# A four-layer graph network: layer 2's self loops put into memory, blocks of its normalisation moved, and the order of layer 3's edge loop changed

## The chip, the cores and the metric

The kernel runs on one core of one Trainium2 chip. The metric is the device time of one launch in microseconds (us). The core's engines are TensorE (PE; its weight loads, PEld, run beside its matmuls), VectorE (DVE), ScalarE (ACT), GpSimd (POOL) and SyncE (SP). Each takes its own instructions in the order in which they were issued and waits on semaphores for what another engine or a transfer has to deliver.

## The reference

A graph of 3125 nodes with 256 features runs through four layers. Each layer normalises x, adds to x the output of a graph attention and of a second mixing branch, and then adds the output of a gated network of experts ("ffn"). There are 50,000 random pairs taken in both directions and one self loop for each node, so 103,125 edges, sorted by target. Two of the attentions matter here.

```python
# layer 2, 4 heads of 64: attention over the edges and, once more, over self loops
src = concatenate([edge_index[0], loop]); dst = concatenate([edge_index[1], loop])
alpha = leaky_relu(a_s[src] + a_d[dst], 0.2)           # per edge and head
coef = softmax of alpha over the edges of one dst
out = relu(segment_sum(coef[:, :, None] * h[src], dst) + bias)
y = out + x
return (y - mean) * rsqrt(var + 1e-5) * gamma + beta   # per node

# layer 3, 8 heads of 32: three terms per edge, each of 4 kinds, weighted by an edge mask
e = (left(src, mask) + right(dst, mask) + em(edge_attr_16, mask)) / 3.0
e = where(e > 0, e, 0.2 * e)
a = softmax of e over the edges of one dst
rst = segment_sum(feat_src[src] * a[:, :, None], dst)
```

## The kernel before

**Units.** Nodes are taken in 25 tiles of 125 (`TP` = 125, `NT` = 25) as targets and in 25 tiles of 128 (`NS`) as sources. The edges stand in 806 columns of 128 (`NE`, `P`), sorted by target. Layers 0 to 2 do their attention densely: a matrix of edge counts, `count_d`, one byte for each pair of source and target, is built once in memory, and `weigh` (L2058) multiplies a tile of it by the exponentials of the scores.

**Layer 2, `dense`.** Four chunks of targets, (0, 6), (6, 6), (12, 6) and (18, 7) in tiles, each go over 25 source tiles. A step loads a tile of counts (`count_tile`, L2064), adds the identity where the tile crosses the diagonal (L2072, because layer 2 counts each self loop once more than the graph has it), makes four weighted tiles on DVE (L2061), and multiplies them on PE (L2316, L2321). Work of the chunk before is woven in, one piece at a step (`next(work, None)`): first `turned`, the transposing and scaling of its tiles, then `gnn2_blocks` (L1297), the addition, normalisation and residual for three or four tiles at a time. PE, DVE and ACT are in an order written out by hand there. The blocks of the last chunk are returned as `tail` and run within the expert network of layer 2 (FFN2, `ffn2` from L1396), three pieces after each expert of the first group of tiles. FFN2 also calls `between()` once, which works on weights of layer 3.

**Layer 1's second attention**, which has one head, runs in the loop `go`, over seven groups of targets (`ONES`) and 25 source tiles. It reads the same `count_d`, and it is the last reader of it before layer 2.

**Layer 3, `edge_attention`.** Here work goes by edges: 101 steps (`steps`) of eight columns (`SC`), the last with six. `columns(t)` (L1842) gives for each target tile the range of columns in which its edges may lie: the range that even spacing gives, with a margin of four columns at both sides. `here[i]` lists the target tiles, one or two, whose range meets step i. The parts of a step are:

- `load`: target numbers (`row`), edge features (`ef`) and masks by DMA on SP's queue, three steps ahead.
- `gather` (L2592): eight indirect DMAs on POOL's queue bring the rows of the sources into `z_edge` (four buffers).
- `targets` (L2605): for each tile of the step, DVE compares target numbers with node numbers into `hot`, which has two buffers.
- `products` (L2617, L2620): PE sums the edge features' term and `er` times `hot` into `p_m`; ACT copies it to `m_sb` (L2622).
- `turn` (L2627): PE transposes `m_sb` into `p_e`.
- `weights` (L2635 to L2651): on DVE `l`, twice, and `e`, twice; ACT's exponential `near_e` (L2643); DVE's one-hot matrices `oh` (L2647, three buffers); and DVE's multiplication of the gathered rows by the weights, in place in `z_edge` (L2651).
- `sums` (L2660): PE multiplies `oh` and `z_edge` column by column into `p_acc`, one accumulator for a target tile.
- `divide`: DVE divides a finished tile by its sum and adds it to x.

The loop over i issues load(i+3), products(i), sums(i-2), gather(i+1), weights(i-1), targets(i+1), divide(i-2) and turn(i), with two calls of `piece()` between, which bring in work of layer 3's mixing branch and its expert network as it becomes ready. PE and DVE take this order as it is written (`manual_schedule`); ACT's order is left to the scheduler.

Of the kernel before, what the change touches and what calls it, by code (L numbers as in the profile page):

```python
# [2 lines left out]

# [60 lines left out]
class Net:  # L64
# [1231 lines left out]

    def gnn2_blocks(self, x, xn, att, weights, t0, nt):  # L1297

        nc = self.nc
        for b in range(t0, t0 + nt, 3 if nt == 6 else 4):  # L1300
            n = min(3 if nt == 6 else 4, t0 + nt - b)
            gamma, beta = (r[:, None, :].to_broadcast([TP, n, C]) for r in weights)
            a, xs = att[:, b:b + n, :], x[:, b:b + n, :]
            nc.vector.tensor_add(a, a, xn[:, b:b + n, :])
            nc.gpsimd.tensor_add(xs, xs, beta)
            yield
            mv = self.moments(a, (0, n))
            yield
            rstd = self.norms.tile([TP, 4], F32, name="rstd")
            nc.scalar.activation(rstd[:, :n], mv[:, :n, 1], AF.Sqrt, bias=self.eps5[:TP], scale=1.0)  # L1310
            yield
            nc.vector.reciprocal(rstd[:, :n], rstd[:, :n])
            back = self.norms.tile([TP, 4], F32, name="back")
            nc.vector.scalar_tensor_tensor(back[:, :n], mv[:, :n, 0], -1.0, rstd[:, :n], op0=OP.mult, op1=OP.mult)
            for t in range(n):
                nc.scalar.activation(a[:, t, :], a[:, t, :], AF.Identity, bias=back[:, t:t + 1], scale=rstd[:, t:t + 1])
            yield
            nc.vector.tensor_mul(a, a, gamma)
            nc.vector.tensor_add(xs, xs, a)
            yield  # L1320
# [75 lines left out]
    def ffn2(self, x, xn, xT, weights, tail=None, between=None):  # L1396
        nc, tc = self.nc, self.tc
        E = 8
        with ExitStack() as s:
# [56 lines left out]
            def aside(i, e):  # L1456
                if i + 1 < len(GROUPS):
                    t0, nt = GROUPS[i + 1]
                    if e == 0:
                        mv[i] = self.moments(x, GROUPS[i + 1])  # L1460
                    if e == 1:
                        self.normed(xn, x, GROUPS[i + 1], mv[i])
                    if e == 2:
                        self.transposed(ps, xT, xn, groups=[GROUPS[i + 1]])
                    if e == 3:
                        raw[i] = self.exponents(ws, self.scores(ws, ps, xT[:, :, t0 * TP:(t0 + nt) * TP], nt, wr, br))
                    if e == 4:
                        wfs[i + 1] = self.shares(ws, raw[i])
                if e == 5:
                    turn_weights(i)  # L1470
                if e == 6:
                    add_biases(i)
                if tail and i == 0:
                    for _ in range(3):
                        next(tail, None)
                if between and (i, e) == (1, 4):
                    between()
# [144 lines left out]
class Dense(Net):  # L1622
# [219 lines left out]
    def columns(self, t):  # L1842

        return max(0, t * TP * 33 // P - MARGIN), min(NE, -(-(t + 1) * TP * 33 // P) + MARGIN)

# [217 lines left out]

    def count_tile(self, w, t, d0, n, loops, width=875):  # L2064
        nc = self.nc
        K = min(P, N - t * P)
        a = w.tile([P, width], U8, name="a")
        nc.sync.dma_start(a[:K, :n], self.count_d[t, :K, d0:d0 + n])
        if loops:
            lo, hi = max(t * P, d0), min(t * P + K, d0 + n)  # L2070
            if lo < hi:
                nc.vector.tensor_add(a[:K, lo - d0:hi - d0], a[:K, lo - d0:hi - d0], self.ident[:K, lo - t * P:hi - t * P])  # L2072
        return a, K

    def dense_pairs(self, att, nodes, then):
# [7 lines left out]
        with ExitStack() as s:  # L2083
# [48 lines left out]
            def near_counts(n):  # L2132
                c, _ = near[n // NS]
                counts[n] = self.count_tile(wa, n % NS, c * TP, nq, False, nq)

# [116 lines left out]

    def dense(self, nodes, scaled, then, finish=None, loops=False, early=None, first=None, onward=None, **side):

# [5 lines left out]
        with ExitStack() as s:  # L2260
# [36 lines left out]
            with tc.manual_schedule(engines={mybir.EngineType.PE, mybir.EngineType.DVE, mybir.EngineType.Activation}):  # L2297
                for i in (0, 2):
                    ask(0, i)
                for c, (t0, nt) in enumerate(chunks):  # L2300
# [5 lines left out]
                    for t in range(NS):  # L2306
                        a, K = self.count_tile(wa, t, d0, n, loops)
                        pts = [self.weigh(wp, qs[i][:K, :n], bar[:K, t, i:i + 1], a, n, K) for i in range(4)]
# [44 lines left out]
    def attention_one(self, x, xT, name, slope, w, load):  # L2353
# [51 lines left out]
        def onward(wq, wa, wp, wo, ps1, ps):  # L2405
# [34 lines left out]
            def weighed(i, t):  # L2440
                t0, nt = ONES[i]
                a, K = self.count_tile(wa, t, t0 * TP, nt * TP, False)
                pts[i, t] = self.weigh(wp, qs[i][:K, :nt * TP], bar[:K, t:t + 1], a, nt * TP, K), K
# [14 lines left out]

            def go(work):
                order = [(i, t) for i in (0, 1) for t in range(ready)] + [(i, t) for i in (0, 1) for t in range(ready, NS)]  # L2460
                order += [(i, t) for i in range(2, len(ONES)) for t in range(NS)]
# [3 lines left out]
                for at in range(len(order) + 4):  # L2465
# [3 lines left out]
                    if at < len(order):  # L2469
# [4 lines left out]
                        if i and t == 14:  # L2474
                            if i == 2:
                                load()
                            if i + 1 < len(ONES):
                                ask(i + 1)
# [10 lines left out]
                    next(work, None)  # L2489
                for _ in work:  # L2490
                    pass
# [34 lines left out]
    def edge_attention(self, x, xT, weights, pieces, then):  # L2526
# [10 lines left out]
        with ExitStack() as s:  # L2537
# [25 lines left out]
            nc.gpsimd.iota(node_sb, pattern=[[TP, NT]], base=0, channel_multiplier=1, allow_small_or_imprecise_dtypes=True)  # L2563
            nc.vector.tensor_copy(node, node_sb)
            work = [pieces(wt, pst)]

# [41 lines left out]
            def products(i):  # L2608

                p_m = ps.tile([P, 2 * P], F32, name="p_m")  # L2610
                for t in [None] + here[i]:
                    for q in range(4):
# [6 lines left out]
                        elif strips(i, t)[0] <= q < strips(i, t)[1]:  # L2619
                            nc.tensor.matmul(p_m[s, :], er[:, t, :], hots[i, t][:, qs], start=False, stop=(t == last))  # L2620
                terms[i] = w.tile([P, 2 * P], F32, name="m_sb")
                nc.scalar.activation(terms[i], p_m, AF.Copy)  # L2622

# [54 lines left out]
            last = len(steps)  # L2678
            with tc.manual_schedule(engines={mybir.EngineType.PE, mybir.EngineType.DVE}):
                for i in range(3):  # L2680
# [3 lines left out]
                for i in range(last + 2):  # L2684
                    if i + 3 < last:
                        load(i + 3)
                    if i < last:
                        products(i)
                    if i >= 2:
                        sums(i - 2)  # L2690
                    if i + 1 < last:
                        gather(i + 1)
                    if 1 <= i <= last:
                        weights(i - 1)
                    piece()
                    if i + 1 < last:
                        targets(i + 1)
                    if i >= 2:
                        divide(i - 2)
                    if i < last:  # L2700
                        turn(i)
                    piece()
                while work:
                    piece()
# [490 lines left out]
    def layers(self, x, xn, xT, out, late):  # L3195
# [55 lines left out]
        with tc.tile_pool(name="node2", bufs=1) as ap:  # L3251
            nodes = self.beside(ap, "g2", xT, 4, 0.2, lambda work: self.mix2(x, xn, xT, work, gw[-1]), self.row(ap, "L2_gnn_bias", P))
            tail = self.dense(nodes, lambda t, p, inv: self.gnn2_scaled(att, t, p, inv),
                              lambda t0, nt, ps: self.gnn2_blocks(x, xn, att, gw, t0, nt), loops=True,
                              early=lambda ps: self.ffn2_first(x, xn, xT, ps))
# [147 lines left out]
```

## Time and profile before

| | |
|---|---|
| median of 10 runs | 5135.85 us (5129.56 to 5148.08) |
| the profiled execution's own time | 5138.03 us |
| its span | 5136.2 us |
| mean granted PE clock | 0.948 of full speed |
| busy share of the span | PE 91%, PEld 55%, DVE 66%, ACT 32%, POOL 30% |
| layer 1's one-head loop | about 2150 to 2400 us |
| layer 2's dense loop | 2818 to 3257 us, chunks of 98.9, 107.0, 108.8 and 123.7 us |
| FFN2 | 3257 to 3838 us |
| layer 3's edge loop | 3876 to 4934 us |
| end of layer 3 | to 5136 us |

The span is that of one profiled execution, from the first to the last instruction; all durations are from it. "Busy" leaves out the time in which an engine waits. In rows of the profile `out<-in` gives the tiles that an instruction writes and reads, "x" how many there were, and "idle before" the time in which the engine stood still ahead of them, with what ended it. L with a number is a line of the kernel before.

### The profile page before, as it was taken

How to read it: one execution, taken by the hardware profiler on the slowest of the kernel's cores; microseconds unless marked ns; L12 is line 12 of the kernel's file. 1: busy time of each engine (PE TensorE's matmuls, PEld its weight loads, DVE VectorE, ACT ScalarE, POOL GpSimd, SP SyncE). 2: the span in 40 equal slices, each digit the busy share in tenths (PEclk: the TensorE clock that was granted, in tenths of full speed). 3: DMA queues.
4: the chain of work that ended last, by engine and by line, in shares of the span. 5: the costliest groups of instructions: out<-in, count | busy, mean ns of one | idle time of the engine just before them, and what ended most of it. 6: DMA issues, size and time to landing. Idle time of an engine off the chain costs nothing. (4 is left out here: it accounts for less than half of the span.)

```text
span 5136.2 us, 74838 instructions
## 1 busy us (share of the span) xinstructions
PE 4654.4 (91%) x28141; PEld 2824.8 (55%) x28141; DVE 3387.1 (66%) x5768; ACT 1666.2 (32%) x2861; POOL 1521.3 (30%) x1413
## 2 busy tenths in 40 slices
PE   6798999969899899999998999999996787889878
PEld 4564433448656444488555433455664565555567
DVE  6988887855635888755334999522236887777843
ACT  2668877731243011110332011233331102323221
POOL 1107866824300000000001000000006777777733
PEclk8899999979999999999999999999998898999989
DMA  4866544532300111121000111200005566666645
GB/s 94 82 59 168 161 126 142 145 114 65 103 1 3 40 42 38 31 46 38 3 16 23 32 42 31 71 10 0 1 18 158 164 184 179 169 178 173 192 140 172
DMA packets 351142, 443.50 MB, mean 86 GB/s; under 512 B 145052, under 2 KB 270256, under 8 KB 350329
## 3 DMA queue, kind: packets, MB, share of 16 engines
q1 hardware_dynamic: 266790, 222.80, 17.9%
q0 software_dynamic: 55024, 175.53, 12.0%
q10 hardware_dynamic: 28959, 40.29, 2.5%
q8 instruction: 228, 3.74, 0.3%
q14 instruction: 141, 1.15, 0.1%
HBM read 384.87 MB, written 56.78 MB: 86 GB/s over the span
## 5 line engine op out<-in xcount | busy, mean ns | idle before, releaser
L2061 DVE SCALAR_TENSOR_TENSOR pt<-q_head,bar,a 128x750 f32<-128x750 f32 (+4 forms) x975 | 889.1, 964 | 154.3 <-PE acc L2448 88.2
L2592 POOL DMA_INDIRECT z_edge<-tab,src_i x806 | 774.8, 961 | 303.9 <-issue 209.8
L2316 PE MATMUL acc<-pt,zs 128*32 128x375 f32 (+1 forms) x6400 | 637.1, 496 | 22.4 <-DVE pt L2061 14.5
L2187 POOL TENSOR_TENSOR pt_far<-pt_far,a_far 128x1125 f32<-128x1125 f32 (+1 forms) x200 | 476.4, 2383 | 277.1 <-DMA a<-count_d 147.7
L2660 PE MATMUL p_acc<-z_edge,oh 128*125 128x264 f32 x2044 | 525.3, 416 | 3.1 <-DVE z_edge L2651 3.1
L2142 DVE SCALAR_TENSOR_TENSOR pt<-q_here,bar,a 128x1000 f32<-128x1000 f32 (+1 forms) x384 | 455.8, 1249 | 46.3 <-DMA a<-count_d 17.7
L2660 PEld LDWEIGHTS p_acc<-z_edge,oh 128*125 128x125 f32 x2044 | 405.8, 203 | 131.0 <-issue 41.6
L2156 PE MATMUL p_n<-pt,zs 128*64 128x500 f32 (+1 forms) x1600 | 404.6, 597 | 28.5 <-DVE pt L2142 28.2
L2316 PEld LDWEIGHTS acc<-pt,zs 128*32 128x32 f32 x6400 | 224.5, 110 | 349.0 <-issue 246.9
L2321 PE MATMUL acc<-pt,zs 128*32 128x375 f32 (+2 forms) x3200 | 352.2, 491 | 0.0
L1436 DVE SCALAR_TENSOR_TENSOR x<-p_y,sm,x 125x256 f32<-125x256 f32 x200 | 96.6, 483 | 381.0 <-PE p_y L751 381.0
L2448 PE MATMUL acc<-xn,pt 128*125 128x257 f32 (+1 forms) x1250 | 283.5, 382 | 10.5 <-DVE pt L2061 9.9
L2448 PEld LDWEIGHTS acc<-xn,pt 128*125 128x125 f32 (+1 forms) x1250 | 229.3, 187 | 56.8 <-DVE pt L2061 14.7
L2156 PEld LDWEIGHTS p_n<-pt,zs 128*64 128x64 f32 (+1 forms) x1600 | 155.2, 137 | 190.6 <-issue 93.9
L1420 ACT ACTIVATE h<-p_tr,bn 128x500 f32<-128x500 f32 (+1 forms) x224 | 161.4, 722 | 296.5 <-PE p_tr L751 296.5
L2201 PE MATMUL p_f<-pt_far,zs 128*64 128x375 f32 (+1 forms) x1200 | 244.2, 489 | 8.5 <-POOL pt_far L2187 8.3
L2185 ACT ACTIVATE pt_far<-q_log,log_s 128x1125 f32<-128x1125 f32 (+1 forms) x200 | 244.8, 1224 | 20.4 <-PE p_f L2201 17.4
L2186 ACT ACTIVATE pt_far<-pt_far,log_s 128x1125 f32<-128x1125 f32 (+1 forms) x200 | 247.1, 1235 | 6.5
L2651 DVE TENSOR_TENSOR z_edge<-z_edge,near_e 128x2112 f32<-128x2112 f32 (+1 forms) x101 | 236.4, 2341 | 16.0 <-ACT near_e L2643 15.9
L2620 PE MATMUL p_m<-hot,er 125*32 125x256 f32 x1046 | 103.5, 445 | 141.9 <-DVE hot L2605 140.4
L2321 PEld LDWEIGHTS acc<-pt,zs 128*32 128x32 f32 (+1 forms) x3200 | 127.1, 109 | 154.4 <-issue 147.1
L2647 DVE SCALAR_TENSOR_TENSOR oh<-near,dst_f 128x1000 f32<-128x1000 f32 (+2 forms) x149 | 153.3, 1044 | 63.2 <-PE p_acc L2660 63.2
(583 smaller groups left out, 7466.1 us busy)
## 6 DMA issues: line engine op xcount, KB each, us to landing
a<-count_d SPq DMA_DIRECT2D x384, 125.0 KB
a_far<-far_d SPq DMA_DIRECT2D x96, 281.2 KB
row<-dst_row SPq DMA_DIRECT2D x101, 224.0 KB
a<-count_d SPq DMA_DIRECT2D x144, 93.8 KB
ef<-in_edge_s SPq DMA_DIRECT2D x101, 128.0 KB
z_edge<-tab,src_i POOLq DMA_INDIRECT x806
count_d<-stage SPq DMA_DIRECT2D x12, 781.2 KB
q_head<-q_g ACTq DMA_DIRECT2D x24, 375.0 KB
```

Of the source, the lines that this page charges most:

```text
L2061: self.nc.vector.scalar_tensor_tensor(pt[:K, :n], q, bar, a[:K, :n], op0=OP.max, op1=OP.mult)
L2142: nc.vector.scalar_tensor_tensor(pt[:K], q[:K], bar[:K, t, h:h + 1], a[:K].rearrange("p (j n) -> p j n", j=2), op0=OP.max, op1=OP.mult)
L2156: nc.tensor.matmul(accs[u][64 * j:64 * j + 64, :M * TP], zs[:K, t, h * W:h * W + 64], pt[:K, j, :], start=(t == 0), stop=(t == NS - 1))
L2185: nc.scalar.activation(f[:K], logs[u, i][:K], AF.Relu, bias=log_s[:K, 0, t, h])
L2186: nc.scalar.activation(f[:K], f[:K], AF.Exp, bias=log_s[:K, 1, t, h], scale=1.0 - 0.2)
L2187: nc.gpsimd.tensor_tensor(f[:K], f[:K], a[:K], OP.mult)
L2201: nc.tensor.matmul(far_accs[u][b][64 * i:64 * i + 64, :n], zs[:K, t, z:z + 64], fs[i][:K, b * n:(b + 1) * n], start=(t == 0), stop=(t == N ...
L2316: nc.tensor.matmul(acc[i // 2][r:r + 32, b, :b1 - b0], zs[:K, t, i * W + f:i * W + f + 32], pts[i][:K, b0:b1], **st)
L2321: nc.tensor.matmul(acc[2][32 * i:32 * i + 32, b, :b1 - b0], zs[:K, t, z:z + 32], pts[i][:K, b0:b1], **st)
L2448: nc.tensor.matmul(banks[i, j], pt[:K, j * TP:(j + 1) * TP], zs[:K, t, :], start=(t == 0), stop=(t == NS - 1))
L2592: nc.gpsimd.indirect_dma_start(out=zs[i][:, j, :], out_offset=None, in_=table, in_offset=bass.IndirectOffsetOnAxis(ap=src[:, c0 + j:c0 + j ...
L2660: nc.tensor.matmul(acc[t], ohs[i, t][:, k - a, :], zs[i][:, k - c0, :HW], start=(k == cols[t][0]), stop=(k == cols[t][1] - 1))
```

## The change

- **Self loops of layer 2.** `count_tile` adds the identity no more. `add_loops` loads the diagonal blocks of `count_d` in the one-head loop of layer 1, at group 2, adds the identity to them at group 4 and stores them after that loop. The counts in memory then have layer 2's self loops.
- **Blocks of layer 2's normalisation.** Which blocks run behind which chunk is now a table: (9, 3), (12, 3) and (15, 3) go into the tail. The tail runs in FFN2, three pieces after each expert of the first group and two of the second; `between()` is called after the eighth expert of the second group in place of the fifth, with the rest of the tail ahead of it.
- **Columns.** The margin of `columns` is computed from the spread of the edges' places, two to four columns.
- **Layer 3's loop.** `sums(i - 2)` stands ahead of `products(i)`, and `targets(i + 1)` ahead of `weights(i - 1)`. The copy to `m_sb` is a part of its own, `copied(i)`, behind `weights(i - 1)`. A one-element exponential (`soon`) ends each step. ACT's order is by hand here too.

```diff
@@ -1294,11 +1295,10 @@
         for i in range(4):
             nc.scalar.activation(att[:, t, i * 64:(i + 1) * 64], p[:, i // 2, 64 * (i % 2):64 * (i % 2) + 64], AF.Relu, scale=inv[:, i:i + 1])
 
-    def gnn2_blocks(self, x, xn, att, weights, t0, nt):
-
-        nc = self.nc
-        for b in range(t0, t0 + nt, 3 if nt == 6 else 4):
-            n = min(3 if nt == 6 else 4, t0 + nt - b)
+    def gnn2_blocks(self, x, xn, att, weights, t0):
+
+        nc = self.nc
+        for b, n in {0: ((0, 3), (3, 3)), 6: ((6, 3),), 18: ((9, 3), (12, 3), (15, 3), (18, 4), (22, 3))}.get(t0, ()):
             gamma, beta = (r[:, None, :].to_broadcast([TP, n, C]) for r in weights)
             a, xs = att[:, b:b + n, :], x[:, b:b + n, :]
             nc.vector.tensor_add(a, a, xn[:, b:b + n, :])
...
@@ -1470,10 +1470,12 @@
                     turn_weights(i)
                 if e == 6:
                     add_biases(i)
-                if tail and i == 0:
-                    for _ in range(3):
+                if tail and i < 2:
+                    for _ in range(3 if i == 0 else 2):
                         next(tail, None)
-                if between and (i, e) == (1, 4):
+                if between and (i, e) == (1, 7):
+                    for _ in tail:
+                        pass
                     between()
 
             order = [(i, e) for i in range(len(GROUPS)) for e in range(E)]
...
@@ -1841,7 +1843,10 @@
 
     def columns(self, t):
 
-        return max(0, t * TP * 33 // P - MARGIN), min(NE, -(-(t + 1) * TP * 33 // P) + MARGIN)
+        def margin(b):
+            return min(MARGIN, max(2, math.ceil(3.2 * math.sqrt(32 * TP * b * (NT - b) / NT) / P)))
+
+        return max(0, t * TP * 33 // P - margin(t)), min(NE, -(-(t + 1) * TP * 33 // P) + margin(t + 1))
 
     def counts(self, pieces, later):
 
...
@@ -2061,16 +2066,28 @@
         self.nc.vector.scalar_tensor_tensor(pt[:K, :n], q, bar, a[:K, :n], op0=OP.max, op1=OP.mult)
         return pt
 
-    def count_tile(self, w, t, d0, n, loops, width=875):
-        nc = self.nc
+    def count_tile(self, w, t, d0, n, width=875):
         K = min(P, N - t * P)
         a = w.tile([P, width], U8, name="a")
-        nc.sync.dma_start(a[:K, :n], self.count_d[t, :K, d0:d0 + n])
-        if loops:
-            lo, hi = max(t * P, d0), min(t * P + K, d0 + n)
-            if lo < hi:
-                nc.vector.tensor_add(a[:K, lo - d0:hi - d0], a[:K, lo - d0:hi - d0], self.ident[:K, lo - t * P:hi - t * P])
+        self.nc.sync.dma_start(a[:K, :n], self.count_d[t, :K, d0:d0 + n])
         return a, K
+
+    def add_loops(self, w):
+
+        nc = self.nc
+        whole = N // P
+        left = N - whole * P
+        a = w.tile([P, NS, P], U8, name="own_a")
+        own = (a[:, :whole, :], dview(self.count_d, 0, [[N, P], [P * N + P, whole], [1, P]]))
+        last = (a[:left, whole, :left], dview(self.count_d, whole * (P * N + P), [[N, left], [1, left]]))
+        for rows, at in (own, last):
+            nc.gpsimd.dma_start(rows, at)
+        yield
+        nc.vector.tensor_add(own[0], own[0], self.ident[:, None, :].to_broadcast([P, whole, P]))
+        nc.vector.tensor_add(last[0], last[0], self.ident[:left, :left])
+        yield
+        for rows, at in (own, last):
+            nc.gpsimd.dma_start(at, rows)
 
     def dense_pairs(self, att, nodes, then):
 
...
@@ -2457,6 +2474,7 @@
                     nc.vector.scalar_tensor_tensor(x[:, t0 + j, :], acc[:, :C], inv, x[:, t0 + j, :], op0=OP.mult, op1=OP.add)
 
             def go(work):
+                own = self.add_loops(w)
                 order = [(i, t) for i in (0, 1) for t in range(ready)] + [(i, t) for i in (0, 1) for t in range(ready, NS)]
                 order += [(i, t) for i in range(2, len(ONES)) for t in range(NS)]
                 both = [b for k in range(3) for b in half(k)]
...
@@ -2474,6 +2492,8 @@
                         if i and t == 14:
                             if i == 2:
                                 load()
+                            if i in (2, 4):
+                                next(own)
                             if i + 1 < len(ONES):
                                 ask(i + 1)
                     for i, a, b in ends.pop(at, ()):
...
@@ -2487,7 +2507,7 @@
                         if t == NS - 1:
                             ends.setdefault(at + 2, []).append((i, a, b))
                     next(work, None)
-                for _ in work:
+                for _ in chain(work, own):
                     pass
 
             return go
...
@@ -2562,6 +2582,7 @@
             node_sb = w.tile([TP, NT], F32, name="node")
             nc.gpsimd.iota(node_sb, pattern=[[TP, NT]], base=0, channel_multiplier=1, allow_small_or_imprecise_dtypes=True)
             nc.vector.tensor_copy(node, node_sb)
+            soon = wt.tile([1, 1], F32, name="soon")
             work = [pieces(wt, pst)]
 
             def piece():
...
@@ -2618,8 +2639,12 @@
                                              start=True, stop=(last is None))
                         elif strips(i, t)[0] <= q < strips(i, t)[1]:
                             nc.tensor.matmul(p_m[s, :], er[:, t, :], hots[i, t][:, qs], start=False, stop=(t == last))
-                terms[i] = w.tile([P, 2 * P], F32, name="m_sb")
-                nc.scalar.activation(terms[i], p_m, AF.Copy)
+                terms[i] = p_m
+
+            def copied(i):
+                m_sb = w.tile([P, 2 * P], F32, name="m_sb")
+                nc.scalar.activation(m_sb, terms[i], AF.Copy)
+                terms[i] = m_sb
 
             def turn(i):
                 p_e = ps.tile([P, 2, P], F32, name="p_e")
...
@@ -2676,7 +2701,7 @@
 
 
             last = len(steps)
-            with tc.manual_schedule(engines={mybir.EngineType.PE, mybir.EngineType.DVE}):
+            with tc.manual_schedule(engines={mybir.EngineType.PE, mybir.EngineType.DVE, mybir.EngineType.Activation}):
                 for i in range(3):
                     load(i)
                 gather(0)
...
@@ -2684,22 +2709,26 @@
                 for i in range(last + 2):
                     if i + 3 < last:
                         load(i + 3)
+                    if i >= 2:
+                        sums(i - 2)
                     if i < last:
                         products(i)
-                    if i >= 2:
-                        sums(i - 2)
                     if i + 1 < last:
                         gather(i + 1)
+                    if i + 1 < last:
+                        targets(i + 1)
                     if 1 <= i <= last:
                         weights(i - 1)
+                    if i < last:
+                        copied(i)
                     piece()
-                    if i + 1 < last:
-                        targets(i + 1)
                     if i >= 2:
                         divide(i - 2)
                     if i < last:
                         turn(i)
                     piece()
+                    if i < last:
+                        nc.scalar.activation(soon, self.eps5[:1], AF.Exp)
                 while work:
                     piece()
```

The calls of `count_tile` and `gnn2_blocks` drop their last argument.

More of the change, by code (lines that the diff above doesn't have):

```diff
@@ L2 @@
 from itertools import chain
+import math
 import numpy as np
@@ L2133, in near_counts @@
                 c, _ = near[n // NS]
-                counts[n] = self.count_tile(wa, n % NS, c * TP, nq, False, nq)
+                counts[n] = self.count_tile(wa, n % NS, c * TP, nq, nq)
             def near_weigh(n):
@@ L2251, in dense_pairs, with dense @@
                     ends = [e for e in ends if next(e, self) is not self]
-    def dense(self, nodes, scaled, then, finish=None, loops=False, early=None, first=None, onward=None, **side):
+    def dense(self, nodes, scaled, then, finish=None, early=None, first=None, onward=None, **side):
         nc, tc = self.nc, self.tc
@@ L2306, in dense @@
                     for t in range(NS):
-                        a, K = self.count_tile(wa, t, d0, n, loops)
+                        a, K = self.count_tile(wa, t, d0, n)
                         pts = [self.weigh(wp, qs[i][:K, :n], bar[:K, t, i:i + 1], a, n, K) for i in range(4)]
@@ L2441, in weighed @@
                 t0, nt = ONES[i]
-                a, K = self.count_tile(wa, t, t0 * TP, nt * TP, False)
+                a, K = self.count_tile(wa, t, t0 * TP, nt * TP)
                 pts[i, t] = self.weigh(wp, qs[i][:K, :nt * TP], bar[:K, t:t + 1], a, nt * TP, K), K
@@ L3253, in layers @@
             tail = self.dense(nodes, lambda t, p, inv: self.gnn2_scaled(att, t, p, inv),
-                              lambda t0, nt, ps: self.gnn2_blocks(x, xn, att, gw, t0, nt), loops=True,
+                              lambda t0, nt, ps: self.gnn2_blocks(x, xn, att, gw, t0),
                               early=lambda ps: self.ffn2_first(x, xn, xT, ps))
```

## The prediction

> **What bounds the kernel now.** Only two stretches of the program are touched for long: layer 2's dense loop (2818 to 3257 us, the four chunks of twenty-five steps) and layer 3's edge loop (3876 to 4934 us, 101 steps). I read first the busy times in windows cut at those borders, the columns being window, length, then busy us and instructions of PE, PEld, DVE, ACT and POOL, the granted PE clock, the DMA share and GB/s.
>
> ```profile
> core 0: us, PE busy (x) PEld busy (x) DVE busy (x) ACT busy (x) POOL busy (x), PEclk, DMA share, GB/s
> 2818.10:2917.00 98.90, 98.68 (x1204) 42.43 (x1207) 95.91 (x107) 1.71 (x4) 0.00 (x0) 0.98 0.16 48
> 2917.00:3024.00 107.00, 105.99 (x1226) 41.44 (x1226) 103.82 (x141) 13.19 (x39) 0.00 (x0) 1.00 0.14 38
> 3024.00:3132.80 108.80, 107.06 (x1224) 40.81 (x1225) 104.59 (x141) 11.89 (x38) 0.00 (x0) 1.00 0.14 40
> ...
> 3876.40:4933.60 1057.20, 882.68 (x5028) 600.13 (x5027) 811.40 (x1187) 246.71 (x466) 777.23 (x812) 0.91 0.61 172
> ```
>
> In the dense chunks PE and DVE are both nearly full: the second and third chunk are 8.1 and 9.9 us longer than the first, and DVE's busy time grew by 7.9 and 8.7 with them. DVE work added there is paid almost one to one. In the edge loop nobody is full: a step is 1057.2/101 = 10.47 us, PE is busy 83% of it, DVE 77%, POOL 74%. Second, then, POOL's waits around that stretch (total us, times, longest).
>
> ```profile
> POOL z_edge L2592 <- issue: 209.8, 688, 0.4
> ...
> POOL z_edge L2592 <- PE p_acc L2660: 16.2, 26, 3.2
> ```
>
> POOL's gathers set the pace: 806 of them, each 0.96 us busy and 0.30 of "issue", 1.26 x 8 = 10.1 us a step, and their waits for freed buffers are small (11 are over 0.3 us, 20.8 us together). Third, the groups by line, for the prices (busy us, mean ns, then idle before and what ended it).
>
> ```profile
> L2660 PE MATMUL p_acc<-z_edge,oh 128*125 128x264 f32 x2044 | 525.3, 416 | 3.1 <-DVE z_edge L2651 3.1
> ...
> L2651 DVE TENSOR_TENSOR z_edge<-z_edge,near_e 128x2112 f32<-128x2112 f32 (+1 forms) x101 | 236.4, 2341 | 16.0 <-ACT near_e L2643 15.9
> L2605 DVE TENSOR_TENSOR hot<-row,near 125x1024 f32<-125x1024 int16 (+3 forms) x148 | 156.1, 1081 | 0.0
> L2647 DVE SCALAR_TENSOR_TENSOR oh<-near,dst_f 128x1000 f32<-128x1000 f32 (+2 forms) x149 | 153.3, 1044 | 63.2 <-PE p_acc L2660 63.2
> L2620 PE MATMUL p_m<-hot,er 125*32 125x256 f32 x1038 | 102.9, 445 | 140.7 <-DVE hot L2605 139.2 <-DVE z_edge L2651 1.1
> ...
> L2617 PE MATMUL p_m<-ef,attn_m 16*32 16x256 f32 x800 | 65.6, 399 | 0.0
> ...
> L2640 DVE TENSOR_REDUCE e<-l 128x64 f32<-128x256 f32 (+1 forms) x101 | 60.9, 603 | 3.5
> ...
> L2638 DVE TENSOR_TENSOR l<-l,mask 128x256 f32<-128x256 f32 (+1 forms) x101 | 43.1, 427 | 3.5
> L2635 DVE TENSOR_TENSOR l<-p_e,z_edge 128x256 f32<-128x256 f32 (+1 forms) x101 | 42.4, 420 | 81.1 <-PE p_acc L2660 24.2 <-DMA z_edge<-tab,src_i 21.4 <-PE p_e L2627 21.2
> ...
> L2641 DVE SCALAR_TENSOR_TENSOR e<-e 128x64 f32<-128x64 f32 (+1 forms) x101 | 23.0, 228 | 3.5
> ```
>
> The 0.0 behind L2605 is the row that matters most: today `hot` never waits on DVE. PE waits 139.2 us for `hot`, up to 7.4 at a time, under POOL's pace.
>
> **Three blocks of layer 2 into FFN2.** Blocks (9,3), (12,3), (15,3) leave chunks three and four. A block costs DVE 0.95 for the first add, 3 x (0.40 + 0.18) for the moments, 0.33 for reciprocal and shift, 1.91 for the last two operations: 4.94 us, three are 14.8. Paid one to one by the windows above: -15 (bounds -8, were PE's near-full share the real limit, and -22 with the loops below). In FFN2 PE is busy 567.6 of 581.5 us, so what is hidden there is hidden by PE; but its `p_tr` waits for ACT's `h` four times, 9.1 us, where the two present blocks run. Five blocks: +2 (0 to +5). `between()` only runs three steps later; its result is read after 3838.
>
> **Self loops.** The 27 recorded adds of L2072 at 0.26 to 0.28 us (7 us of DVE over four chunks) go. The first chunk, with seven of them, has PE at 98.7 of 98.9 us, so I count 0 for them. In their place come two loads and two stores on POOL's queue and one add of 3072 elements in the one-head loop (2150 to 2400 us). By the 128x750 row (0.96 us) the add is about 4 us, an estimate; PE is busy 239.7 of those 250 us and weighted tiles are made ahead, so 0, at worst +4. POOL is idle there (0.35 us busy), and the stores have 400 us to land.
>
> **Narrower columns.** 1022 pairs of edge column and tile become 1002, 523 strips 513, 149 pairs of step and tile 146, all at the first and last five tiles. A pair costs PE 525.3/1022 = 0.51 us and DVE 0.15: -10 us of PE, -6 of DVE with the strips. Alone this is hidden by POOL's pace; it enters the chain below as about -0.15 us a step.
>
> **Exponentials.** A dummy Exp at the end of each step draws the table load (L2643, 35 loads of 1283 ns) out of the path from `e` to the multiplication by `near_e`. The trace prices that path's loss at 15.9 us of DVE waiting in the whole loop, under POOL's pace; so 0, at best -16. The Trainium skill's "ScalarE: Activation LUTs", section What ACT_TABLE_LOAD costs, gives 2.66 us for each switch with its drain; 35 of them would make this part -93. The waits of this trace say that most of that is covered already.
>
> **The order in layer 3's loop.** Iteration i on PE is now sums(i-2), products(i), turn(i); on DVE it is targets(i+1), weights(i-1), divide(i-2). Either swap shortens a wait that is there: PE's 139.2 us for `hot`. Together they close a loop, because `hot` has two buffers. Where steps i and i+1 have more than two tiles between them, which is so for 69 of the 100 neighbouring pairs ((1,2) 24, (2,1) 24, (2,2) 21), a `hot` of step i+1 needs a buffer that products(i) reads. Products(i) stand on PE behind sums(i-2). And queued behind the waiting `hot` on DVE are l, l, e, e, oh and the multiplication of step i-1, on which sums(i-1) wait, and behind these products(i+1). Before, targets came after weights and products before sums, so none of this was a circle. In the changed kernel's instruction order 137 of 146 `hot` wait for PE (84 of 149 before).
>
> One turn of the circle, from the rows above: DVE 156.1 + 42.4 + 43.1 + 60.9 + 23.0 + 153.3 + 236.4 = 715.2, or 7.08 us a step; PE 525.3 + 102.9 + 65.6 = 693.8, or 6.87 us; together 13.95, with the narrower columns 13.8, against 10.47 now. 69 x 13.8 = 952. The other 31 steps lie between DVE's busy time (811.4/101 = 8.0 us) and POOL's pace and its present slack (10.3): 248 to 319, and I take the middle, 285. The loop: 1237, +180 (ends 1200, +143, and 1271, +214). What is late next is POOL: its gathers wait for z_edge buffers that sums release, and lose nothing more by it.
>
> PE becomes idler, and here its clock counts. The trace: 3876 to 4355 us, PE 77% busy, clock 0.88; 4600 to 4917, 89% busy, 0.96. At (882.7 - 10)/1237 = 71% the nearest row is 0.88, perhaps 0.87: 0.91/0.87 on 6.87 us is 0.3 a step, 69 times, up to +22, which goes to the upper end. The Trainium skill's "TensorE: Matmul & The Clock Gate", section Part 1: The HAM clock gate, halves the clock after an idle window of about 3.4 us and needs as long to warm up. DVE's part of the circle is 7 us, so by this rule every such step would start cold and lose some 1.7 us, +117 in all. The trace already has pauses of up to 7.4 us (the waits for `hot`) and 0.88 beside them, and speaks for the smaller figure.
>
> **Sum.** -15 + 2 + 0 + 0 + 180 = +167. The profiled execution took 5138.03 us (span 5136.2), 2.2 above the median of 5135.85, well inside the spread of the runs (5129.56 to 5148.08): 5136 + 167 = 5303 us.
>
> **Rivals.** (A) The circle doesn't decide, and the loop falls onto POOL's pace: its waits go (-20.8) and some 5 us of the tail behind the last gather, which is 16 us now: 5136 - 26 - 13 = 5097, faster. For it speaks that POOL bounds today and that PE has 17% of slack; it decides if a step's wait of `hot` stays under about 10.3 - 8.0 = 2.3 us. Against it, sums and products alone are 6.87 us. (B) The circle closes in part: only the second `hot` of a step waits and the first (1.08 us) slips out, and products of the first tile run early; 12.0 to 13.8 us for 69 steps with 8.0 for the rest is 1076 to 1200, +19 to +143 less 13: 5142 to 5266, middle 5200. (C) The circle closes and takes in other work: the pieces of layer 3's hidden layer (DVE 811 - 715 = 96 us, two thirds of it in closed steps, 65) and the colder clock (22): 5303 + 87 = 5390. For it: ACT is in hand order too, so `m_sb` of step i stands behind near_e of step i-1. (D) The narrow columns miss an edge and the general path runs: in the given inputs tile 2's first edge lies in column 63 and its range starts at 61, and so for the rest; chance nil.
>
> **Chances.** The forecast 0.72, C 0.12, B 0.10, A 0.06. A measurement of this kernel tells about 0.2%, 10 us, from no change; A is faster by more, a small part of B within it. The range leaves out A, the lower half of B and what lies above C: 5200 to 5390.
>
> **What would show it.** Right: the loop is near 1240 us; `hot`, 0.0 now, waits hundreds of us on DVE for PE's products; sums wait over 100 us for the multiplied z_edge (3.1 now); gathers wait for sums in most steps, 150 us or more; the loop's clock is at or under 0.88; chunks three and four are near 104 and 114 us. Wrong: `hot` waits under 2.3 us a step and the gathers keep 1.26 us. If chunks three and four don't shorten, or FFN2 grows by over 5 us, the smaller terms are wrong.

## The result

The changed kernel takes 5377.32 us (median of 8 runs, 5371.31 to 5384.18) where the kernel before takes 5138.06 (28 runs): ratio 1.0464, interval 1.0455 to 1.0473, 239 us slower. The forecast was 5303 us, 165 above before, with a range up to 5390: direction and mechanism held, and the loss was half as large again.

The windows of the changed kernel, cut at the same borders (window, length, busy us of PE, PEld, DVE, ACT and POOL, clock, DMA share, GB/s):

```profile
core 0: us, PE busy (x) PEld busy (x) DVE busy (x) ACT busy (x) POOL busy (x), PEclk, DMA share, GB/s
2814.70:2912.10 97.40, 97.35 (x1204) 56.08 (x1207) 94.91 (x102) 1.71 (x4) 0.00 (x0) 0.98 0.16 48
2912.10:3019.00 106.90, 105.91 (x1226) 41.41 (x1223) 102.44 (x134) 13.20 (x39) 0.00 (x0) 1.00 0.14 38
3019.00:3122.00 103.00, 102.54 (x1226) 40.57 (x1226) 98.69 (x123) 10.03 (x34) 0.00 (x0) 1.00 0.15 42
3122.00:3236.40 114.40, 114.37 (x1220) 41.71 (x1218) 106.52 (x117) 8.37 (x30) 0.00 (x0) 1.00 0.08 22
3855.70:5172.90 1317.20, 988.15 (x4969) 661.67 (x4969) 806.67 (x1182) 245.27 (x560) 776.82 (x812) 0.83 0.48 138
```

The dense chunks are 1.5, 0.1, 5.8 and 9.3 us shorter, 16.7 together. From the end of the dense loop to the first gather it was 619.9 us (3256.5 to 3876.4) and is 619.3 (3236.4 to 3855.7), so FFN2 swallows its three blocks. The edge loop, from the first gather to the last division, was 1057.2 us and is 1317.2 (3855.7 to 5172.9): +260. The rest, ahead of the dense loop and behind the edge loop, is -4.5, and the sum, +238, is the difference of the spans (5136.2 and 5374.4). In the last line above the loop's work is what it was (POOL 777 us for 777, DVE 807 for 811), PE is busy 105 us longer with less of it, and the clock fell from 0.91 to 0.83.

The waits of the changed kernel in that loop (total us, times, longest):

```profile
engine line waited for: us in total, times, longest us
...
DVE hot L2626 <- PE p_m L2641: 426.1, 75, 13.6
POOL z_edge L2613 <- PE p_acc L2685: 287.3, 73, 10.8
...
PE p_e L2652 <- ACT m_sb L2646: 181.1, 74, 10.6
...
PE p_acc L2685 <- DVE z_edge L2676: 99.5, 62, 3.0
```

`hot`, which never waited, waits 75 times and 426 us for products; the gathers wait 73 times for sums, 287 us where it was 16; the sums wait 99.5 us for the multiplied `z_edge`, where it was 3.1. These are the three arcs of one circle. One turn of it can be read off the timeline (start, us, engine, line, operation, and in brackets the idle time before with its releaser):

```profile
start us, us, engine line op out<-in xcount [idle before <-releaser]
4310.03 2.34 DVE L2676 TENSOR_TENSOR z_edge<-z_edge,near_e 128x2112 f32<-128x2112 f32 x1
...
4312.43 5.87 PE L2685 MATMUL p_acc<-z_edge,oh 128*125 128x264 f32 x16 [2.11 <-DVE z_edge L2676]
...
4318.23 0.63 PE L2638 MATMUL p_m<-ef,attn_m 16*32 16x256 f32 x8
...
4318.80 1.07 PE L2641 MATMUL p_m<-hot,er 125*32 125x256 f32 x10
4319.53 2.35 DVE L2626 TENSOR_TENSOR hot<-row,near 125x1024 f32<-125x1024 int16 x2 [5.60 <-PE p_m L2641]
...
4323.49 1.19 DVE L2672 SCALAR_TENSOR_TENSOR oh<-near,dst_f 128x1000 f32<-128x1000 f32 x1
...
4324.25 0.69 PE L2652 MATMUL p_e<-ident,m_sb 128*128 128x128 f32 x2 [4.38 <-ACT m_sb L2646]
4324.60 2.34 DVE L2676 TENSOR_TENSOR z_edge<-z_edge,near_e 128x2112 f32<-128x2112 f32 x1
...
4327.00 0.80 PE L2685 MATMUL p_acc<-z_edge,oh 128*125 128x264 f32 x1 [2.06 <-DVE z_edge L2676]
```

The multiplication ends at 4312.4, the sums start at once and end at 4318.3, the products follow and release both `hot` after 5.60 us of waiting, then come l, l, e, e, `oh` and the next multiplication, which ends at 4326.9: 14.6 us a turn, and at no moment of it do PE's sums and DVE's chain run side by side. PE stands idle for 4.4 us ahead of the transposes and for 2.1 us ahead of the sums. Its granted clock in the same turn, cut where it changes (columns as in the windows above):

```profile
4309.80:4316.60 6.80, 4.69 (x12) 3.31 (x13) 4.03 (x7) 0.00 (x0) 4.83 (x6) 0.50 0.96 304
4316.60:4323.40 6.80, 3.27 (x26) 1.64 (x24) 3.77 (x6) 0.00 (x0) 3.91 (x4) 1.00 0.62 181
4323.40:4330.20 6.80, 3.89 (x9) 2.77 (x10) 3.54 (x3) 0.61 (x3) 3.91 (x5) 0.50 0.52 154
```

The clock is whole or half, and the sums of this turn and of the next begin at half. From the first to the last gather it stands at half in 65 stretches, 457 of 1293 us; in the kernel before in 29 stretches, 181 of 1041 us.

I took the time from the end of each such multiplication to the end of the next, and sorted it by how many tiles the two steps have whose products and `hot` fall in it (mean us; the numbers of pairs are those between the loop's ends):

| kernel | (1,1) x29 | (1,2) x24 | (2,1) x24 | (2,2) x21 |
|---|---|---|---|---|
| changed | 9.3 | 15.0 | 14.2 | 14.6 |
| hot4 | 10.7 | 9.3 | 10.5 | 10.4 |
| hot3 | 10.1 | 9.3 | 8.5 | 14.6 |
| targets_back | 10.2 | 8.8 | 10.3 | 11.6 |
| products_first | 9.9 | 9.4 | 10.1 | 11.4 |

In the changed kernel the 69 pairs with more than two tiles take 1007 us, 14.6 each, and the others 9.3. A closed turn holds on average 7.13 us of the seven DVE operations of the circle and 7.44 us of PE's sums and products, 14.57 together: it is their sum.

### The profile page after: what moved, and what is told of

Its sections match the earlier page's. It is cut to its first block, busy times and chain, and to the rows that moved or that the text cites. A ratio compares the mean times of both kernels' runs of the same rounds, so it can differ in the third digit from the quotient of the medians.

```text
span 5374.4 us, 74907 instructions
## 1 busy us (share of the span) xinstructions
PE 4739.3 (88%) x28081; PEld 2889.1 (54%) x28081; DVE 3376.7 (63%) x5736; ACT 1664.1 (31%) x2954; POOL 1527.3 (28%) x1417
## 3 DMA queue, kind: packets, MB, share of 16 engines
q0 software_dynamic: 55312, 176.32, 11.4%
## 4 chain that ended last, share of the span: by engine, by line
PE 69%; DVE 12%; issue 5%; ACT 4%; POOL 3%; DMA 3%; DVEq 0%; ACTq 0%; SPq 0%; POOLq 0%
PE acc L2333 10%; PE p_acc L2685 9%; PE p_tr L752 8%; PE p_n L2173 5%; PE acc L2465 5%; PE acc L2338 5%; PE p_y L752 4%; PE p_q L752 4%; PE p_h L752 4%; PE p_f L2218 3%; DVE z_edge L2676 3%; PE p_a L752 2%; PE p_t L752 2%; PE p_kvt L752 2%; POOL z_edge L2613 1%
## 5 line engine op out<-in xcount | busy, mean ns | idle before, releaser
L2685 PE MATMUL p_acc<-z_edge,oh 128*125 128x264 f32 x2004 | 597.2, 464 | 99.7 <-DVE z_edge L2676 99.5
L2333 PE MATMUL acc<-pt,zs 128*32 128x375 f32 (+1 forms) x6400 | 617.0, 495 | 20.8 <-DVE pt L2066 13.6
L2685 PEld LDWEIGHTS p_acc<-z_edge,oh 128*125 128x125 f32 x2004 | 456.2, 232 | 225.6 <-DVE z_edge L2676 113.7
L2626 DVE TENSOR_TENSOR hot<-row,near 125x1024 f32<-125x1024 int16 (+2 forms) x146 | 157.3, 1088 | 426.2 <-PE p_m L2641 426.1
L2668 ACT ACTIVATE near_e<-e 128x64 f32<-128x64 f32 (+1 forms) x101 | 22.8, 226 | 756.8 <-DVE e L2666 756.8
L2652 PE MATMUL p_e<-ident,m_sb 128*128 128x128 f32 x202 | 52.1, 347 | 186.5 <-ACT m_sb L2646 181.1
```

The lines of the kernel that those rows point to most:

```text
L2333: nc.tensor.matmul(acc[i // 2][r:r + 32, b, :b1 - b0], zs[:K, t, i * W + f:i * W + f + 32], pts[i][:K, b0:b1], **st)
L2685: nc.tensor.matmul(acc[t], ohs[i, t][:, k - a, :], zs[i][:, k - c0, :HW], start=(k == cols[t][0]), stop=(k == cols[t][1] - 1))
```

## The experiments

The first theory is the circle. Its rival is ACT's new order by hand: the copy to `m_sb` of step i stands behind `near_e` of step i-1, and PE waits 181 us for it. The kernels ran in three sets, each on a chip of its own beside the kernel before. That kernel took 5153 us on the chip of the first set and 5365 and 5366 on those of the second and the third, so ratios are compared, and edge loops only within a set, or between the first set and the result, whose chips are 0.3% apart (5153 and 5138 us).

**hot4: four buffers for `hot`, orders as changed.**

The edit, by its buffer numbers alone:

```diff
-  rows bufs=4, efs bufs=4, masks bufs=5, node_sb bufs=2, hots bufs=2, ohs bufs=3
+  rows bufs=3, efs bufs=3, masks bufs=4, node_sb bufs=1, hots bufs=4, ohs bufs=2
```

> Circle theory: with four buffers no hot of step i+1 has to wait for the products of step i (two tiles a step at most), so hot's 426 us of waiting on DVE go to nearly nothing, the sums no longer wait 100 us for the multiplied z_edge, and the edge loop falls from about 1293 us to the gathers' own pace, 101 x 10.2 = 1030 to 1045. Time 5095 us, 5080 to 5120, 3% under the changed kernel and some 0.8% under the kernel before. Rival theory (the copy to m_sb, which ACT now makes behind near_e of the step before, holds the transposes: 181 us of PE waiting): ACT's order is untouched, so the time stays above 5300 us. Second rival (a colder clock alone): 5340 or more, as nothing makes PE busier. The room comes from three buffers for row and ef, four for mask, two for oh, one for node; they can only cost time.

Ratio 0.9941 (0.9925 to 0.9958), 5122 us against 5153. Its waits:

```profile
engine line waited for: us in total, times, longest us
...
POOL z_edge L2613 <- PE p_acc L2685: 16.2, 32, 4.0
...
DVE hot L2626 <- PE p_m L2641: 1.6, 3, 1.3
```

426 us became 1.6, and the gathers run from first to last in 1029.7 us where the changed kernel needed 1293 on the chip of the result. Buffers alone take the whole loss away, and with them the order that the change brought costs 10 us at most (5112 in targets_back below). The second rival, a colder clock alone, falls too: nothing was added to PE, and its clock in that stretch is 0.91.

**hot3: three buffers**, the same edit with `hots bufs=3` and `ohs` and `node_sb` as they were.

> Circle theory: three buffers open the 48 pairs of neighbouring steps with three tiles and leave the 21 with four closed. By the measured 14.6 us of a closed step and POOL's 10.3 for the others the loop is at most 21 x 14.6 + 80 x 10.3 = 1130 us, and less where the neighbours catch up through the four z_edge buffers: 1050 to 1130. Time 5115 to 5215 us, most likely near 5140; slower than with four buffers. hot on DVE waits well under 150 us, in some 21 steps. Rival (m_sb behind near_e): above 5300 us.

Ratio 0.9981 (0.9971 to 0.9991), 5141 us, 19 above hot4. Its waits:

```profile
DVE hot L2626 <- PE p_m L2641: 103.3, 32, 11.8
```

The table above has the sharper answer: with three buffers the pairs of three tiles fall to 9.3 and 8.5 us, those of four stay at 14.6 in the mean (their median is 13.4, where it was 14.3). The number of buffers against the number of tiles decides which steps are closed, as the prediction counted. That the gathers still take only 1046 us from first to last fits the expectation that four `z_edge` buffers let open steps make good for one closed step in five; no run varies those buffers.

**targets_back and products_first: one of the two swaps undone.**

```diff
 targets_back                      products_first
-    targets(i + 1)               -    sums(i - 2)
     weights(i - 1)                    products(i)
     copied(i); piece()           +    sums(i - 2)
+    targets(i + 1)
```

> targets(i+1) goes back behind weights(i-1) on DVE, sums stay ahead of products, ACT stays in hand order. Circle theory: the multiplication of z_edge no longer stands behind hot, so nothing returns to its start; the loop runs at the gathers' pace, 1030 to 1045 us, the wait of PE for hot (139 us before) is gone too, as sums lie between. Time 5095 us, 5080 to 5115. Rival (m_sb behind near_e): the ACT order is the same as in the changed kernel, above 5300 us.

> products(i) goes back ahead of sums(i-2) on PE, targets stay ahead of weights, ACT stays in hand order. Circle theory: products no longer wait behind the sums, so hot's buffer is free early; loop at the gathers' pace, 1035 to 1050 us, time 5100 us, 5085 to 5125. Rival (m_sb behind near_e): above 5300 us.

Ratios 0.9925 (0.9908 to 0.9941) and 0.9931 (0.9914 to 0.9947). In targets_back the loop's window between first and last gather reads:

```profile
3870.70:4895.70 1025.00, 879.61 (x4933) 592.29 (x4932) 799.98 (x1169) 247.33 (x554) 779.46 (x806) 0.91 0.65 176
```

No gap between two gathers is over 0.6 us, and POOL's 806 pitches of 1.27 us fill the window. With either swap alone the loop is no slower than before (1025 and 1022 us from first to last gather, where it was 1041); only both together close the circle. ACT's order is the changed one in all four kernels, so the rival falls: in targets_back PE's wait for `m_sb` shrinks by itself from 181 to 51 us, so most of it was an effect. These two are the fastest versions in this set; the changed kernel did not run on its chip.

**old_loop: layer 3's order as before, all else as changed.**

In words:

```diff
-    (loop of the changed kernel, copied(i), soon, ACT by hand)
+    (loop of the kernel before)
```

> The changed kernel with the step order of layer 3 as it was (products, sums, weights, targets; ACT left to the scheduler; no dummy exponential). It prices all the rest: blocks in FFN2, self loops, columns. By the chunks of the changed kernel's trace (97.4, 107.0, 103.0, 114.4 against 98.9, 107.0, 108.8, 123.7) and FFN2 unchanged: -16.7 us, and nothing from the columns under the gathers' pace: ratio 0.9967, 0.996 to 0.9975. Rival (FFN2 gives the blocks' time back): 0.999 to 1.001.

Ratio 0.9969 (0.9959 to 0.9978): 16.8 us of 5365, where 16.7 were expected. The chunks are 97.7, 107.0, 103.1 and 114.4 us.

**columns_only: the kernel before with the narrower columns.**

```diff
-    max(0, t * TP * 33 // P - MARGIN), ...
+    max(0, t * TP * 33 // P - margin(t)), ...
```

> The kernel before with the narrower columns alone. Pace theory: 10 us less of PE and 6 of DVE lie under the gathers' pace: 0 to -5 us, ratio 0.999 to 1.0005. Rival (PE's time in the loop comes through): -10 us, ratio 0.998.

Ratio 0.9992 (0.9983 to 1.0002): nothing that can be told from zero.

**after_again, targets_back_again, no_soon, no_soon_again.** The second set's chip raised the question what is due to the chip, so the third set ran these side by side. no_soon is targets_back without the line `nc.scalar.activation(soon, self.eps5[:1], AF.Exp)`.

> targets_back without the dummy exponential. Cover theory: the table load returns to the path from e to z_edge, DVE waits 15 to 60 us more for near_e over the loop, but the gathers still set the pace and hardly wait: within 5 us of targets_back, ratio to before 0.992 to 0.9945. Rival (every switch is paid, 35 x 1.28 = 45 us or more): ratio 1.000 or above.

> The changed kernel itself, on the chip of the three runs beside it, because the four runs before these were on a chip on which the kernel before took 5365 us. Ratio 1.046 as before if the chip is like the first ones; on a chip with a colder clock in the loop more than 1.03.

> The version that beats both kernels, again, with targets(i+1) behind weights(i-1). Ratio 0.9925 as before, 0.991 to 0.994, if the chip is like the first ones.

> targets_back without the dummy exponential, beside it on one chip. Cover theory: the gathers set the pace, so within 5 us of targets_back (ratio between the two 0.999 to 1.001). Rival (the switches of the table are paid, 35 x 1.28 us or more): 45 us or more above targets_back, as the first try, 1.0098 on the other chip, would suggest if the chip isn't its cause.

no_soon gave 1.0098 (1.0075 to 1.0120) on the second chip, far from its expectation; on the third, no_soon_again 1.0048 (1.0032 to 1.0063) and targets_back_again 1.0050 (1.0033 to 1.0068), 5395 and 5399 us. So on the third chip the dummy exponential is worth nothing that shows. That the chip also made the 1.0098 is argued only: targets_back was not run on the second chip, and why the same kernel without the exponential is 21 us slower there than on the third is open. Without the exponential the table loads stand again on the path from `e` to `near_e`:

```profile
L2667 ACT ACT_TABLE_LOAD x35 | 44.9, 1283 | 43.3 <-DVE e L2665 19.4 <-issue 19.4 <-DVE e L2664 4.2
```

That is 35 loads of 1283 ns, 45 us, on the path; with the exponential the same 35 stand at `soon`, behind it, and the difference in time is 4 us the other way. The changed kernel itself was 1.0318 (1.0289 to 1.0346) there, 142 us above targets_back_again on the same chip: the circle costs there too, but less.

targets_back_again missed its expectation. On this chip it is slower than the kernel before, and its gathers take 1292.8 us for 1024.9. Here is ACT in one of its steps:

```profile
3903.87 0.23 ACT L2668 ACTIVATE near_e<-e 128x64 f32<-128x64 f32 x1 [4.14 <-issue]
3935.32 0.38 ACT L2646 ACTIVATE m_sb<-p_m 128x256 f32<-128x256 f32 x1 [31.22 <-remote]
```

The last product of that step is recorded as ended by 3904.5, and the copy of `p_m` starts 31 us later, with DVE and PE idle as well. PE has 13 pauses of over 8 us in that loop, 182 us together, and one of 12 us in targets_back's on the first chip; old_loop on the second chip has 5, 53 us. What holds PE there the trace doesn't say ("remote"), and no run here takes it apart; why the new order meets more such pauses than the old stays open as well.

**warm6 and warm4: idle matmuls in PE's pauses.** They ask why a closed step takes 14.6 us and not 13.8. The edit of warm4, shortened:

```diff
 def turn(i):
     p_e = ...
+    for _ in range(3): nc.tensor.matmul(p_e, self.ident, gw[:, 0, :2 * P], start=True, stop=True)
     (two transposes)
+    for _ in range(1): nc.tensor.matmul(p_m, self.ident, gw[:, 0, :2 * P], start=True, stop=True)
```

warm6 has three in the second place.

> The changed kernel with six idle matmuls a step (results overwritten unread): three ahead of turn(i) and three behind it, where PE stands idle in a closed step (2.5 us for m_sb, 2 us for z_edge). It asks why a closed step takes 14.6 us and not the 13.8 of the prediction. Clock theory: PE is idle too long, the loop's clock is 0.83 and a column of the sums 0.60 us where it was 0.51; busier, the clock comes back to 0.90 or more, a column to 0.53, a closed step to about 14.0: 69 x 0.6 = 41 us less, 5336 us (5310 to 5360). Rival (the excess is pieces and waiting between engines in the circle): the added 3.6 us of PE a step only stand in the way, clock or not: 5377 to 5440, with the column's price unchanged or without effect on the step.

> The changed kernel with four idle matmuls a step, three ahead of turn(i) and one behind it, beside the changed kernel on one chip. With six, on the other chip, the clock of the loop was 0.95 and a column of the sums 0.47 us, but the sums waited for z_edge only 10 us, so that the fillers had become part of the circle. Clock theory: with four they end inside the idle time; a column 0.50 to 0.54 us, a closed step 13.8 to 14.1 us in place of 14.6, 30 to 50 us under after_again. Rival (the excess is pieces and waiting between engines): no less than after_again, although the clock rises.

warm6 took 1.0118 (1.0099 to 1.0136) on the second chip, where the changed kernel didn't run, so it can't be weighed. warm4 beside after_again, on one chip: 1.0167 (1.0152 to 1.0182) and 1.0318, 5455 and 5541 us. More work for PE made the kernel 85 us faster, where 30 to 50 were expected. Loop windows and sums, first after_again, then warm4:

```profile
3877.30:5314.90 1437.60, 987.17 (x4854) 658.34 (x4855) 792.41 (x1148) 238.00 (x543) 773.82 (x806) 0.79 0.45 126
...
L2685 PE MATMUL p_acc<-z_edge,oh 128*125 128x264 f32 x1957 | 583.8, 465 | 89.5 <-issue 57.3 <-DVE z_edge L2676 32.2
```

```profile
3869.00:5218.80 1349.80, 1078.63 (x5638) 742.15 (x5639) 792.87 (x1148) 235.86 (x541) 775.16 (x806) 0.91 0.48 134
...
L2689 PE MATMUL p_acc<-z_edge,oh 128*125 128x264 f32 x2004 | 511.8, 414 | 70.0 <-issue 54.7 <-DVE z_edge L2680 15.2
```

The clock goes from 0.79 to 0.91 and a column of the sums (two records) from 0.597 us (583.8/978.5) to 0.511. The medians of closed steps, in the order (1,2), (2,1), (2,2), fall from 18.2, 14.2 and 15.1 to 16.9, 12.7 and 13.7, by 1.2 to 1.5 us, more than the 0.5 to 0.8 expected. But after_again also had more of the long pauses (9 of over 8 us, 125 us, against 4, 46 us). So it is shown that filling the pauses raises the clock and lowers the column's price; how much of the 85 us is clock and how much pauses is not.

## Why the prediction was right, and where it fell short

**The circle.** Right in every arc: `hot` has two buffers, the pairs with more than two tiles are closed, and each swap alone is harmless on the chip of the first set. Of the signs that it named, `hot` waits 426 us, the gathers wait for sums 73 times and 287 us, the clock is 0.83, and chunks three and four are 103.0 and 114.4 us; the sums wait 99.5 us, at the edge of the 100 named, and the loop is 1317 us and not near 1240. Rival A's price for a loop without it, 5097 us, is what targets_back gave: 0.9925 x 5138 = 5100. Rival B (half open) is out by its price: all three closed classes lie at 14.2 to 15.0, where it had 12.0 to 13.8. What it describes does happen in the 24 pairs (1,2): the first `hot` starts 1.2 us after the multiplication (median), beside the sums, and only the second waits. These turns aren't shorter, because their sums are longer, 12.25 columns against 8 in the other two classes.

**The size.** The sum said +180 for the loop; it is +260. Two terms of the working account for the 80, and a third held.

- *The turn of the circle, 13.8 us.* It is 14.6, 0.8 x 69 = 55 us. DVE's 7.08 held. PE's 6.87 was mis-sized, because the prices came from a loop with a warmer clock: a column of the sums is 0.597 us in the changed kernel (592.6/992), where it was 0.514 (525.3/1022).

```profile
L2685 PE MATMUL p_acc<-z_edge,oh 128*125 128x264 f32 x1984 | 592.6, 465 | 99.7 <-DVE z_edge L2676 99.5
```

With 1002 columns over 101 steps the sums are 5.92 us a step, the two kinds of products 1.47 (83.6 + 63.8 over 100), so PE 7.39, and the turn 14.4 to 14.5; some 0.1 is left for the steps between engines. The clock was in the text, but by the rows of before as 0.87, worth +22, and only in the upper end. It is 0.83. The rows had PE at 77% at their idlest; at 75% and with pauses in every turn it fell further. The price was read off the rows' mean clock, and such a mean lies over stretches at whole and at half clock, as the windows of the turn show; the sums of a closed turn come right behind a pause.
- *The open steps.* 285 us for 31, 9.2 each: 9.3 measured. Nothing to mend.
- *The ends of the loop.* The sum counted 100 steps and was compared with the loop from the first gather to the last division, which has the filling and the emptying as well: 1057.2 less 1032.7 for the 100 steps of before is 24 us, and 22 in the changed kernel. That was an oversight.

By the prediction's estimate from the Trainium skill's "TensorE: Matmul & The Clock Gate", section Part 1: The HAM clock gate, every closed step would lose 1.7 us. The trace agrees in kind, with a clock that switches between whole and half, but the estimate was too dear: PE's sums lost 0.8 a step, the products gained 0.2.

**The range.** The forecast's own upper end, with the open steps at 10.3 us and the colder clock, is 5136 + 214 - 13 + 22 = 5359. The measured 5377 lies within the stated range only because that was drawn up to rival C, and this is luck.

**Rival C** (pieces and `m_sb` inside the circle, 5390) came out near the measured time for a wrong reason: of its 87 us, 65 were pieces, and the closed step has hardly 0.1 us of room for them. The clock, its other 22, was a true term, and too small.

**The small terms.** Dense loop: -16.7 for -15, of which -15.1 in chunks three and four (-5.8 and -9.3), from which the blocks and their share of the self loops' adds went, and -1.5 in the first, from which only such adds went. FFN2: +2 expected, -0.6. Self loops: the one add takes 3.35 us, estimated at 4, and it is hidden: the matmuls of layer 1's one-head loop, which end at about 2455 us and not at 2400, span 305.0 us before (2150.5 to 2455.5) and 305.1 in the changed kernel. Columns: 0, as said. Exponentials: 0, as said, but shown on the third chip alone, where the gathers don't set the pace. By an estimate from the Trainium skill's "ScalarE: Activation LUTs", section What ACT_TABLE_LOAD costs, which gives 2.66 us a switch, the 35 would make 93 us. no_soon_again, 4 us under targets_back_again, shows none of that paid on this path.

## What to carry to other kernels

Before two engines' orders are changed together, follow each buffer around: a step that waits for a buffer, what is queued behind it on its engine, who needs that, and whether that ends at the buffer's reader. If the way closes, the loop runs at the sum of the engines' times and not at the larger; one buffer more, or one swap fewer, opens it. And price a chain through TensorE with the clock that the chain itself will leave, not with that of the loop before.

## What the runs showed that was not expected

- With PE 75% busy and standing idle for 2 to 4 us twice in a turn, its clock fell to half about once a turn, and a column of the sums took 16% longer (0.597 us for 0.514). Useless matmuls in those pauses brought the column back (0.511), and the kernel was 85 us faster, part of it perhaps from fewer long pauses.
- The same kernel took 5138 to 5153 us on some chips and 5365 us on two others, nearly all of it in the edge loop (by columns_only, which takes the same time as the kernel before to 0.1%: 1246 us between first and last gather for 1041 in the profile of before, 205 of the 223 us between the two spans; its dense chunks are as before). There TensorE stood still for up to 34 us at a time (after_again; 30 in targets_back_again) behind its own recorded matmuls, and the order of versions changed: targets_back is 0.75% faster than the kernel before on one chip and 0.5% slower on another. old_loop gained its 0.3% on the slower kind; it wasn't run on the other. What differs between the chips stays open.
